# A selective scan's projections as high and low parts in float32r passes, with d, u and gate projected once

## The chip, the cores and the metric

The kernel runs on one core of one Trainium2 chip. The metric is the device time of one execution in microseconds (us). The fast runs of one kernel on one chip agree here within 0.6%. PE is the matmul engine, DVE the vector engine, ACT the scalar engine, POOL the general-purpose one, SP the one that issues most transfers; PSUM is the matmuls' output memory, SBUF the main one. In the views PEld is PE's weight loads, and a q behind an engine is its sequencer. The granted clock is the share of full speed at which PE was let run, 1.00 or 0.50 at any time in these traces; a mean lies between.

## The reference, cut to what matters

Four images of 64 x 64 tokens with 96 channels go through two layers. Layer 0 is a recurrence with 16 states per channel, whose coefficients are projections of the normed tokens; layer 1 is an attention without a softmax and a quantized feed-forward.

```python
proj = layernorm(groupnorm(x)) @ W_in + b_in             # 96 -> 3*96 + 3*96*16
value, gate, delta, A, Bm, Cm = split(proj)              # u, gate, d; a, b, c per channel and state
# over the 4096 tokens of an image, one after the other:
h = d * (A_t * h) + d * (B_t * u)
y = sigmoid(gate) * sum_over_states(C_t * h)
x = x + y @ W_out + b_out
# layer 1
t = x + attention(layernorm(x));  t = t + feed_forward(layernorm(t))
```

## The kernel before

The 4096 tokens of an image are 8 chunks of 512. A chunk's channels are 3 groups of 32, and a group's 16 states are 4 tiles of (4 states x 32 channels) = 128 partitions by 512 tokens. Per tile there are three projections (a, b, c) and one scan on DVE.

```python
def conv_main(b, i, cg):                       # one group of channels of one chunk
    d_ps = proj(pab, w_d[:, cg, :], "dps", "pab");  nc.scalar.copy(d_sb, d_ps)
    u_ps = proj(pab, w_u[:, cg, :], "ups", "pab")
    nc.vector.tensor_tensor(du, u_ps, d_sb, ALU.mult)
    for sh in range(NSH):                      # 4 tiles of states
        b_ps = proj(pab, w_b[:, cg, sh, :], f"bps{sh}", "pab")
        nc.scalar.copy(bu[:, sh, :], b_ps)
        nc.gpsimd.tensor_tensor(bu[:, sh, :], bu[:, sh, :], du, ALU.mult)
    for sh in range(NSH):
        a_ps = proj(...);  nc.vector.tensor_tensor(da, a_ps, d_sb, ALU.mult)
        nc.vector.tensor_tensor_scan(h[:, sh, :], da, bu[:, sh, :], state, ALU.mult, ALU.add)
        c_ps = proj(...);  nc.vector.tensor_tensor(ch[:, sh, :], c_ps, h[:, sh, :], ALU.mult)
    nc.gpsimd.tensor_tensor(ch[:, 0:2, :], ch[:, 0:2, :], ch[:, 2:4, :], ALU.add)
    nc.gpsimd.tensor_tensor(ys, ch[:, 0, :], ch[:, 1, :], ALU.add)
    # [cut: the state of the last token]

for g in range(N + NCH):                       # schedule; the framework may still reorder
    conv_gate(g); conv_main(g, 0)
    conv_tail(g - 1)                           # output projection, layer norm, Gram matrix
    conv_main(g, 1)
    attn_ffn(of the image before)              # layer 1 of one chunk
    # [cut: loads; in the seventh chunk gn_var, the next image's group-norm statistics]
    conv_front(g + 1)                          # group norm, layer norm, transpose of the next chunk
    conv_main(g, 2)
```

Of the kernel before, what the change touches and what calls it, by code (L numbers as in the profile page):

```python
# [8 lines left out]
F32 = mybir.dt.float32  # L9
F16 = mybir.dt.float16  # L10
F8 = mybir.dt.float8e5  # 5 exponent bits, 2 mantissa bits, infinities: the reference's q_mul
# [4 lines left out]
P = 128  # L16
B, H, W, C = 4, 64, 64, 96
L = H * W                # tokens per image
S = 16                   # states per channel
CA = C + 1               # channels and the row (or column) of ones that carries the biases  # L20
J = 4                    # token 4p + j of a chunk lies on partition p
TC = P * J               # tokens per chunk
NCH = L // TC            # chunks per image
NCG = C // 32            # groups of 32 channels
NSH = S // 4             # groups of 4 states; a scan tile has (state in group, channel in group) on partitions
G = 32                   # groups of the group norm
# [9 lines left out]
def conv_attn_hybrid_kernel(  # L36
# [24 lines left out]
    work = ctx.enter_context(tc.tile_pool(name="work", bufs=2))  # L61
# [6 lines left out]
    # x and out: token b*L + i*TC + J*p + j  # L68
# [9 lines left out]
    def load_x(b, i):  # L78
        t = big.tile([P, J, C], F32, tag="x", name=f"x_{b}_{i}", bufs=2 * NCH + 3)
        nc.sync.dma_start(t, x_v[b, i])  # L80
        xt[b, i] = t
# [12 lines left out]
    # sel[p, cg, c] = 1 where c == 32 cg + p % 32: sums the states of each channel  # L94
# [9 lines left out]
    # D ** -0.5 on the diagonal blocks of the heads, 0 elsewhere  # L104
# [17 lines left out]
    w_b = const.tile([CA, NCG, NSH, P], F32, name="w_b")  # L122
    w_a = const.tile([CA, NCG, NSH, P], F32, name="w_a")
    w_c = const.tile([CA, NCG, NSH, P], F32, name="w_c")
    w_d = const.tile([CA, NCG, P], F32, name="w_d")
    w_u = const.tile([CA, NCG, P], F32, name="w_u")
    w_g = const.tile([CA, C], F32, name="w_g")
    raw = work.tile([CA, A0], F32, tag="h", name="raw0")
    nc.scalar.dma_start(raw[0:C, :], w_in[:, 0:A0])
    nc.scalar.dma_start(raw[C:CA, :], b_in[0:A0].unsqueeze(0))  # L130
    for dst, c0 in ((w_d, 2 * C), (w_u, 0)):
        nc.vector.tensor_copy(
            dst.rearrange("k g (s c) -> k g s c", s=4),
            raw[:, c0 : c0 + C].rearrange("k (g c) -> k g c", g=NCG)
            .unsqueeze(2).to_broadcast([CA, NCG, 4, 32]),
        )
    nc.vector.tensor_copy(w_g, raw[:, C : 2 * C])
    for k, (dst, c0) in enumerate(((w_b, B0), (w_a, A0), (w_c, C0))):
        raw = work.tile([CA, C * S], F32, tag="bu", name=f"raw_{c0}")
        nc.scalar.dma_start(raw[0:C, :], w_in[:, c0 : c0 + C * S])  # L140
        nc.scalar.dma_start(raw[C:CA, :], b_in[c0 : c0 + C * S].unsqueeze(0))
        for cg in range(NCG):
            o = dst[:, cg].rearrange("k h p -> k (h p)").rearrange("k (s c) -> k s c", s=S)
            i_ = raw[:, cg * 32 * S : (cg + 1) * 32 * S].rearrange("k (c s) -> k s c", s=S)
            if (k + cg) % 2:
                nc.vector.tensor_copy(o, i_)
            else:
                nc.scalar.copy(o, i_)
# [10 lines left out]
    # [Wq; bq] transposed, with a unit row that passes bff through  # L159
# [14 lines left out]
    w1_sb = work.tile([P, NK, C], F32, tag="d", name="w1_sb")  # L174
    nc.scalar.dma_start(w1_sb, w1.rearrange("(m p) k -> p m k", p=P))
    w2_sb = work.tile([C, HID], F32, tag="du", name="w2_sb")
# [9 lines left out]
    b1_sb = work.tile([NK, P], F32, tag="da", name="b1_sb")  # L186
# [3 lines left out]
    b1_8 = work.tile([P, NK], F8, tag="xq", name="b1_8")  # L190
    nc.vector.tensor_copy(b1_8, b1_ps, saturate=False)
    nc.vector.tensor_copy(b1_q, b1_8)
    b2_sb = work.tile([P, C], F32, tag="da", name="b2_sb")
    nc.scalar.dma_start(b2_sb, b2.partition_broadcast(P))
    b2_8 = work.tile([P, C], F8, tag="xq", name="b2_8")
# [4 lines left out]
    xnt_t, yg_t, xa_t = [], [], []  # L200
    for r in range(2):
        t = const.tile([CA, TC], F32, tag=f"xnt{r}", name=f"xnt{r}")
        nc.gpsimd.memset(t[C:CA, :], 1.0)
        xnt_t.append(t)
        t = const.tile([CA, TC], F32, tag=f"yg{r}", name=f"yg{r}")
        nc.gpsimd.memset(t[C:CA, :], 1.0)
        yg_t.append(t)
        t = const.tile([P, J, CA], F32, tag=f"xa{r}", name=f"xa{r}")
        nc.gpsimd.memset(t[:, :, C:CA], 1.0)
        xa_t.append(t)  # L210

    def rsqrt(dst, var, eps):
        """dst = (var + eps) ** -0.5"""
        nc.gpsimd.tensor_scalar(dst, var, eps, None, ALU.add)
        nc.gpsimd.tensor_tensor(dst, dst, mhalf[:, : dst.shape[1]], ALU.pow)  # L215

    def layer_norm(dst, src, eps, nm):
        """Per token over the channels; src [P, J, C], dst may be src."""
# [15 lines left out]
    gnm, gnr, gn = {}, {}, {}  # L234
    inv_n = 1.0 / (L * GR)

    def group_sum(ps, dst):
        """Sum over a chunk's J tokens and each group's channels."""
        nc.vector.tensor_reduce(
            dst, ps.rearrange("p (j g r) -> p g j r", j=J, g=G), AX.XY, ALU.add  # L240
        )
# [13 lines left out]
    def gn_var(b):  # L255
        ps = pm.tile([P, J * C], F32, tag="pm", name=f"gnq_{b}")
        for i in range(NCH):
            t = big.tile([P, J, C], F32, tag="gn", name=f"gn_{b}_{i}", bufs=NCH + 2)
# [6 lines left out]
            sq = work.tile([P, J * C], F32, tag="sq", name=f"sq_{b}_{i}")  # L265
            nc.scalar.activation(sq, t.rearrange("p j c -> p (j c)"), AF.Square)
            nc.tensor.matmul(ps, lhsT=ones, rhs=sq, start=(i == 0), stop=(i == NCH - 1))
            gn[b, i] = t
# [8 lines left out]
    def conv_front(b, i):  # L277
        """Group norm, layer norm and transpose of a chunk."""
        t = gn.pop((b, i))
# [8 lines left out]
        for j in range(J):  # L288
            nc.tensor.transpose(ps[:, j, :], t[:, j, :], ident)
        xnt = xnt_t[(b * NCH + i) % 2]  # L290
        nc.scalar.activation(
            xnt[0:C, :].rearrange("c (p j) -> c j p", j=J), ps, AF.Identity,
            bias=bet, scale=gam,
        )

    gate, ysum, state = {}, {}, {}

    def conv_gate(b, i):
        xnt = xnt_t[(b * NCH + i) % 2]
        ps = pab.tile([C, TC], F32, tag="pab", name=f"g_ps_{b}_{i}")  # L300
        nc.tensor.matmul(ps, lhsT=w_g, rhs=xnt, start=True, stop=True)
        g = work.tile([C, TC], F32, tag="gate", name=f"gate_{b}_{i}")
        nc.scalar.activation(g, ps, AF.Sigmoid)
        gate[b, i] = g

    def conv_main(b, i, cg):
        """The recurrence of 32 channels over a chunk."""
        nm = f"{b}_{i}_{cg}"
        xnt = xnt_t[(b * NCH + i) % 2]

        def proj(pool, wt, n, tag):
            ps = pool.tile([P, TC], F32, tag=tag, name=f"{n}_{nm}")
            nc.tensor.matmul(ps, lhsT=wt, rhs=xnt, start=True, stop=True)  # L313
            return ps

        d_ps = proj(pab, w_d[:, cg, :], "dps", "pab")
        d_sb = work.tile([P, TC], F32, tag="d", name=f"d_{nm}")
        nc.scalar.copy(d_sb, d_ps)  # L318
        u_ps = proj(pab, w_u[:, cg, :], "ups", "pab")
        du = work.tile([P, TC], F32, tag="du", name=f"du_{nm}")  # L320
        nc.vector.tensor_tensor(du, u_ps, d_sb, ALU.mult)  # L321

        bu = work.tile([P, NSH, TC], F32, tag="bu", name=f"bu_{nm}")
        for sh in range(NSH):
            b_ps = proj(pab, w_b[:, cg, sh, :], f"bps{sh}", "pab")
            nc.scalar.copy(bu[:, sh, :], b_ps)  # L326
            nc.gpsimd.tensor_tensor(bu[:, sh, :], bu[:, sh, :], du, ALU.mult)  # L327

        h = work.tile([P, NSH, TC], F32, tag="h", name=f"h_{nm}")
        ch = work.tile([P, NSH, TC], F32, tag="ch", name=f"ch_{nm}")  # L330
        st = state.get((b, cg))
        for sh in range(NSH):
            a_ps = proj(pab, w_a[:, cg, sh, :], f"aps{sh}", "pab")
            da = work.tile([P, TC], F32, tag="da", name=f"da{sh}_{nm}")
            nc.vector.tensor_tensor(da, a_ps, d_sb, ALU.mult)  # L335
            nc.vector.tensor_tensor_scan(  # L336
                h[:, sh, :], da, bu[:, sh, :],
                0.0 if st is None else st[:, sh : sh + 1], ALU.mult, ALU.add,
            )
            c_ps = proj(pc, w_c[:, cg, sh, :], f"cps{sh}", "pc")  # L340
            nc.vector.tensor_tensor(ch[:, sh, :], c_ps, h[:, sh, :], ALU.mult)  # L341
        if i < NCH - 1:
            st = small.tile([P, NSH], F32, tag=f"state{cg}", name=f"state_{nm}", bufs=2)
            nc.scalar.copy(st, h[:, :, TC - 1])
            state[b, cg] = st
        nc.gpsimd.tensor_tensor(ch[:, 0:2, :], ch[:, 0:2, :], ch[:, 2:4, :], ALU.add)  # L346
# [176 lines left out]
```

## Time and profile before

The median of the runs taken beside the changed kernel is 2299.5 us (2295.5 to 2304.3), the profiled execution 2306.4 us. By the scans' starts it falls into these stages:

| stage | us |
|---|---|
| to the first scan | 72.6 |
| image 0, eight chunks | 469.2 |
| images 1 to 3, 24 chunks | 1637.8 |
| after the last scan | 126.8 |

The groups that the argument turns on, from the list of costliest groups (count, busy time in all, mean ns of one, then the idle time ahead of them and what ended it):

```profile
L327 POOL TENSOR_TENSOR bu<-bu,du 128x512 f32<-128x512 f32 x384 | 514.7, 1369 | 108.3 <-ACT bu L326 108.1
L336 DVE TENSOR_TENSOR_SCAN h<-da,state,bu 128x512 f32<-128x512 f32 x336 | 478.3, 1423 | 48.4 <-POOL bu L327 35.9
L313 PE MATMUL bps<-xnt,w_b 97*128 97x512 f32 x768 | 401.2, 653 | 0.5 <-DVE du L321 0.3
```

A scan's mean of 1423 ns is a mixture: 1.27 us when it starts with POOL idle (median of 294) and 1.87 us when it starts with POOL active (median of 90). All 82 scans of over 1.4 us end 1.08 us after the end of a POOL instruction (1.078 to 1.086).

### The profile page before, as it was taken

The page shows a single profiled execution, that of the slowest core. Times are in us where ns is not written, and L with a number is a line of the kernel's source. Part 1 is how long each engine was busy: PE and PEld are TensorE (multiplying, and loading weights), DVE is VectorE, ACT ScalarE, POOL GpSimd, SP SyncE. Part 2 cuts the span into 40 slices and gives each one's busy share as a digit, 9 for nine tenths or more (in the row PEclk, how much of TensorE's full clock was granted, in tenths as well). Part 3 has the DMA queues.
Part 4 walks back from the last instruction along what each step waited for, and adds up shares of the span by engine and source line. Part 5 has one row for each costly group of instructions (what it writes and reads, how often), then busy time and mean ns, then how long its engine had stood idle before and what let it go on. Part 6 is the DMA issues. An engine that isn't in the chain of part 4 may idle for free.

```text
span 2306.4 us, 15368 instructions
## 1 busy us (share of the span) xinstructions
PE 1828.3 (79%) x4744; PEld 836.0 (36%) x4744; DVE 1555.9 (67%) x2674; ACT 527.9 (23%) x891; POOL 1117.5 (48%) x898
## 2 busy tenths in 40 slices
PE   2888888878888888878888888887888788888644
PEld 1333333433333333423333333333333333333322
DVE  1677777566777777656767677764776767777633
ACT  1222211211222222222212222212222122222123
POOL 4555545754545445564444554555544454554311
PEclk9899989988988989988889898987988898888755
DMA  3000000000000000000000000000000000000000
GB/s 107 1 0 0 0 0 1 0 0 0 7 7 7 7 1 7 7 7 7 1 7 7 7 7 7 4 0 4 4 4 4 0 4 4 4 4 4 4 11 17
DMA packets 10983, 16.00 MB, mean 7 GB/s; under 512 B 2124, under 2 KB 10609, under 8 KB 10900
## 3 DMA queue, kind: packets, MB, share of 16 engines
q1 hardware_dynamic: 9216, 12.59, 1.7%
q10 hardware_dynamic: 1684, 2.43, 0.4%
q8 instruction: 37, 0.61, 0.1%
q14 instruction: 46, 0.38, 0.1%
HBM read 8.72 MB, written 6.29 MB: 7 GB/s over the span
## 4 chain that ended last, share of the span: by engine, by line
DVE 39%; PE 30%; POOL 14%; issue 11%; ACT 3%; DVEq 0%; POOLq 0%; ACTq 0%
DVE h L336 13%; DVE da L335 6%; PE bps L313 6%; DVE gn L228 5%; DVE xa L228 5%; PE aps L313 5%; DVE ch L341 4%; PE cps L313 4%; PE o_ps L366 3%; POOL ch L346 3%; POOL bu L327 2%; PE y_ps L357 2%; POOL ys L348 2%; PE dps L313 1%; POOL rstd_f L215 1%
## 5 line engine op out<-in xcount | busy, mean ns | idle before, releaser
L313 PE MATMUL cps<-xnt,w_c 97*128 97x512 f32 x768 | 445.2, 664 | 172.0 <-DVE ch L341 171.9
L327 POOL TENSOR_TENSOR bu<-bu,du 128x512 f32<-128x512 f32 x384 | 514.7, 1369 | 108.3 <-ACT bu L326 108.1
L346 POOL TENSOR_TENSOR ch<-ch 128x1024 f32<-128x1024 f32 x96 | 225.5, 2348 | 599.9 <-DVE ch L341 599.9
L336 DVE TENSOR_TENSOR_SCAN h<-da,state,bu 128x512 f32<-128x512 f32 x336 | 478.3, 1423 | 48.4 <-POOL bu L327 35.9
L313 PE MATMUL aps<-xnt,w_a 97*128 97x512 f32 x768 | 445.2, 664 | 0.0
L335 DVE TENSOR_TENSOR da<-aps,d 128x512 f32<-128x512 f32 x384 | 258.6, 674 | 243.7 <-PE aps L313 243.7
L313 PE MATMUL bps<-xnt,w_b 97*128 97x512 f32 x768 | 401.2, 653 | 0.5 <-DVE du L321 0.3
L326 ACT COPY bu<-bps 128x512 f32<-128x512 f32 x384 | 224.7, 585 | 389.3 <-PE bps L313 385.0
L313 PEld LDWEIGHTS cps<-xnt,w_c 97*128 97x128 f32 x768 | 147.8, 210 | 409.9 <-DVE ch L341 291.7
L341 DVE TENSOR_TENSOR ch<-cps,h 128x512 f32<-128x512 f32 x384 | 262.5, 684 | 19.0 <-PE cps L313 1.0
L313 PEld LDWEIGHTS aps<-xnt,w_a 97*128 97x128 f32 x768 | 162.5, 215 | 202.3 <-issue 188.6
L313 PEld LDWEIGHTS bps<-xnt,w_b 97*128 97x128 f32 x768 | 149.9, 207 | 171.3 <-issue 114.8
L457 POOL TENSOR_TENSOR o<-x,yb 128x384 f32<-128x384 f32 x32 | 50.9, 1589 | 292.1 <-DVE yb L453 292.1
L228 DVE TENSOR_SCALAR gn<-gn,mv_c,rstd_c 128x96 f32<-128x96 f32 x128 | 127.3, 1054 | 35.9 <-POOL rstd_c L215 35.9
L228 DVE TENSOR_SCALAR xa<-x,mv_a,rstd_a 128x96 f32<-128x96 f32 x128 | 121.6, 1010 | 29.3 <-POOL rstd_a L215 29.3
L318 ACT COPY d<-dps 128x512 f32<-128x512 f32 x96 | 56.5, 588 | 336.4 <-PE dps L313 336.1
L425 PE MATMUL xq_ps<-ident,xn 128*96 128x128 f32 x128 | 37.8, 394 | 109.3 <-DVE xn L228 109.3
L348 POOL TENSOR_TENSOR ys<-ch 128x512 f32<-128x512 f32 x96 | 121.6, 1266 | 5.5
L375 PE MATMUL gram<-xa 128*97 128x97 f32 x256 | 57.6, 344 | 79.2 <-DVE xa L228 79.2
L357 PE MATMUL y_ps<-ys,sel 128*96 128x512 f32 x192 | 107.1, 701 | 5.7 <-POOL ys L348 5.7
L313 PE MATMUL dps<-xnt,w_d 97*128 97x512 f32 x192 | 105.1, 630 | 0.0
L313 PE MATMUL ups<-xnt,w_u 97*128 97x512 f32 x192 | 102.3, 615 | 0.4
(120 smaller groups left out, 1595.3 us busy)
## 6 DMA issues: line engine op xcount, KB each, us to landing
x<-in_x_dram SPq DMA_DIRECT2D x32, 192.0 KB, 5.4
out_dram<-o SPq DMA_DIRECT2D x32, 192.0 KB, 1.8
raw<-in_L_conv_W_in_dram ACTq DMA_DIRECT2D x3, 576.0 KB, 5.5
w_sb<-in_L_ffn_W_dram ACTq DMA_DIRECT2D x2, 144.0 KB, 2.2
raw<-in_L_conv_W_in_dram ACTq DMA_DIRECT2D x1, 108.0 KB
w_qkv<-in_L_attn_Wqkv_dram ACTq DMA_DIRECT2D x1, 108.0 KB, 2.5
raw<-in_L_conv_b_in_dram ACTq DMA_DIRECT2D x3, 6.0 KB
b_sb<-in_L_ffn_b_dram ACTq DMA_DIRECT2D x1, 48.0 KB
```

Source lines behind the costliest of these rows:

```text
L228: nc.vector.tensor_scalar(dst[:, j, 0:C], src[:, j, :], mv[:, j, 0:1], rstd[:, j : j + 1], ALU.subtract, ALU.mult,)
L313: nc.tensor.matmul(ps, lhsT=wt, rhs=xnt, start=True, stop=True)
L326: nc.scalar.copy(bu[:, sh, :], b_ps)
L327: nc.gpsimd.tensor_tensor(bu[:, sh, :], bu[:, sh, :], du, ALU.mult)
L335: nc.vector.tensor_tensor(da, a_ps, d_sb, ALU.mult)
L336: nc.vector.tensor_tensor_scan(h[:, sh, :], da, bu[:, sh, :], 0.0 if st is None else st[:, sh : sh + 1], ALU.mult, ALU.add,)
L341: nc.vector.tensor_tensor(ch[:, sh, :], c_ps, h[:, sh, :], ALU.mult)
L346: nc.gpsimd.tensor_tensor(ch[:, 0:2, :], ch[:, 0:2, :], ch[:, 2:4, :], ALU.add)
L348: nc.gpsimd.tensor_tensor(ys, ch[:, 0, :], ch[:, 1, :], ALU.add)
L357: nc.tensor.matmul(y_ps, lhsT=sel[:, cg, :], rhs=ysum.pop((b, i, cg)), start=(cg == 0), stop=(cg == NCG - 1),)
L366: nc.tensor.matmul(o_ps[:, j, :], lhsT=yg_v[:, j, :], rhs=w_o, start=True, stop=True)
L375: nc.tensor.matmul(gram[b], lhsT=xa[:, j, :], rhs=xa[:, j, :], start=(i == 0 and j == 0), stop=(i == NCH - 1 and j == J - 1),)
```

## The change

The intent is to unload PE. An fp32 product is two instructions here, 0.86 us together at full clock; a float32r pass is one. The change takes the float32r copy of a value as its high part and what remains as its low part. Activations and weights are split so, and three passes over packed operands (96 high rows and 32 low rows in one tile of 128) give the product of both parts. The bias moves from a row of ones to an ACT bias or the first operand of a fused DVE instruction. d, u and gate are projected once per chunk for all 96 channels, and DMA copies d and d*u onto the four state groups. To make room, many working tiles lose their second buffer (a tile with two buffers can be filled anew while its last content is still read).

```diff
+    def split_weights(dst, src, lo_engine):
+        nc.scalar.copy(dst[0:C, 0], src)                              # high part
+        lo_engine.tensor_tensor(dst[0:C, 1], src, dst[0:C, 0].bitcast(F32), ALU.subtract)
+        # [cut: four copies by DMA fill the packed rows]
# [cut: ten splits (nine for a, b, c, one for d, u, gate), bias rows by 36 one-column matmuls, two instructions each]
 def gn_var(b):
-            sq = work.tile([P, J * C], F32, tag="sq", name=...)       # two buffers
+            sq = work.tile([P, J * C], F32, tag="sq", name=..., bufs=1)
-            gn[b, i] = t                                              # subtracted tile kept
 def conv_front(b, i):
+        nc.gpsimd.tensor_tensor(t, xt[b, i], gnm[b], ALU.subtract)    # done again per chunk
+        nc.scalar.copy(xs[0:C, :], xn)
+        nc.vector.tensor_tensor(lo, xn, xs[0:C, :].bitcast(F32), ALU.subtract)
+        nc.sync.dma_start(xl[0:64, :], lo[0:64, :]);  nc.sync.dma_start(xl[64:P, :], lo[0:64, :])
+        nc.sync.dma_start(xs[C:P, :], lo[64:C, :])
+    def project(pool, tag, nm, b, i, wt, m):
+        for n, mv in enumerate((xs, xs, xl)):
+            nc.tensor.matmul(ps, lhsT=wt[:, n], rhs=mv, start=(n == 0), stop=(n == 2))
 def conv_gate(b, i):
+        # d = ACT(dps + bias); du = DVE((ups + bias) * d); gate = sigmoid(gps + bias)
+        for cg in range(NCG):
+            for nm, src in (("d4", d), ("du4", du)):
+                for s in range(4):
+                    nc.sync.dma_start(t[s * 32 : (s + 1) * 32, :], src[cg * 32 : (cg + 1) * 32, :])
# [cut: conv_main: bu, h, ch as single tiles; da and ch fused with the bias; ys by three POOL additions]
 # schedule
-            conv_gate(b, i)
             conv_main(b, i, 0)
 ...
             conv_front(*divmod(g + 1, NCH))
+            conv_gate(*divmod(g + 1, NCH))
         if g < N:
             conv_main(b, i, 2)
```

## The prediction

> **What bounds the kernel now.** I read the page's busy table first, then the slices, then the stages by windows, then the timelines of single engines inside one chunk.

> ```profile
> span 2306.4 us, 15368 instructions
> PE 1828.3 (79%) x4744; PEld 836.0 (36%) x4744; DVE 1555.9 (67%) x2674; ACT 527.9 (23%) x891; POOL 1117.5 (48%) x898
> DVE 39%; PE 30%; POOL 14%; issue 11%; ACT 3%; DVEq 0%; POOLq 0%; ACTq 0%
> ```

> No engine is full, and the chain that ended last passes through DVE, PE and POOL by turns: the kernel is a relay. So the question is not which engine the change unloads but which hand-overs it shortens.

> The timeline of VectorE gives the stages by the scans' starts. The first scan starts at 72.6 us, the ninth chunk's first at 541.8, the last scan ends at 2179.6. That is a prologue of 72.6 us, image 0 with 469 (eight chunks), images 1 to 3 with 1638 (24 chunks, now with the attention and feed-forward of the image before), and a tail of 127. One ordinary chunk of image 2 runs from 1231.9 to 1298.2. The windows view cut at its scans (columns: us, then PE, PEld, DVE, ACT, POOL busy, the granted clock, DMA share and GB/s):

> ```profile
> 1231.90:1242.30 10.40, 7.86 (x19) 2.91 (x18) 10.15 (x10) 0.01 (x1) 4.54 (x3) 1.00 0.00 0
> 1242.30:1258.80 16.50, 13.74 (x38) 7.66 (x37) 8.11 (x18) 3.70 (x7) 9.82 (x8) 0.79 0.00 1
> 1258.80:1267.60 8.80, 7.92 (x25) 3.77 (x24) 8.59 (x11) 0.57 (x2) 0.00 (x0) 1.00 0.00 0
> 1267.60:1281.90 14.30, 10.84 (x26) 4.27 (x24) 10.07 (x29) 4.69 (x10) 10.92 (x10) 0.88 0.00 1
> 1281.90:1291.70 9.80, 7.20 (x27) 3.38 (x27) 9.70 (x14) 3.56 (x4) 1.09 (x1) 0.83 0.00 0
> 1291.70:1298.20 6.50, 6.50 (x17) 2.91 (x16) 2.12 (x5) 3.27 (x7) 6.26 (x5) 1.00 0.21 61
> 1231.90:1298.20 66.30, 54.07 (x144) 24.91 (x143) 48.74 (x83) 15.81 (x27) 32.63 (x26) 0.90 0.02 6
> ```

> Rows 1, 3 and 5 are the recurrences of the three channel groups: DVE is nearly full there (29 us). Rows 2, 4 and 6 lie between them (37.3 us): there POOL makes the next b*u, PE the projections, and layer 1 and the norms pass. The recurrence itself is DVE-bound; the other half of the chunk is chains.

> The second thing to see is what POOL does to DVE. First a scan with POOL busy, then POOL at that time, then a scan with POOL idle:

> ```profile
> 1095.22 2.27 DVE L336 TENSOR_TENSOR_SCAN h<-da,bu 128x512 f32<-128x512 f32 x1 [0.34 <-POOL bu L327]
> ...
> 1093.91 5.86 POOL L327 TENSOR_TENSOR bu<-bu,du 128x512 f32<-128x512 f32 x4
> ...
> 1061.59 1.28 DVE L336 TENSOR_TENSOR_SCAN h<-da,state,bu 128x512 f32<-128x512 f32 x1
> ...
> 1070.09 1.03 POOL L215 TENSOR_TENSOR rstd_f<-rstd_f,mhalf 128x4 f32<-128x4 f32 x1
> 1071.15 1.05 DVE L228 TENSOR_SCALAR xn<-x,mv_f,rstd_f 128x96 f32<-128x96 f32 x4 [3.25 <-POOL rstd_f L215]
> ...
> 1073.82 4.93 POOL L327 TENSOR_TENSOR bu<-bu,du 128x512 f32<-128x512 f32 x4
> 1073.88 4.94 DVE L228 TENSOR_SCALAR gn<-gn,mv_c,rstd_c 128x96 f32<-128x96 f32 x4 [0.88 <-POOL rstd_c L215]
> ```

> Four normalisations take 1.05 us alone and 4.94 beside four POOL products: each waits for one product to end. Of all scans, the 90 that start with POOL active have a median of 1.87 us and end 1.08 us after POOL's instruction; the other 294 take 1.27. A product is 1.26 us alone.

> [...]da and ch, which have one input in PSUM, stay near 0.68 us. [...]The trace has fp32, two instructions per product, a product every 0.86 us at full clock[...]. [...]the trace has 684 for ch. [...]the trace has 1.8 us for a 192 KB store and 0.34 us of issue each.

> **The change part by part.**
> PE. Before, each channel group makes 14 projections: 14 x 0.86 = 12.0 us, three times a chunk, plus the gate: 37 us. [...]But PE is waited on only at hand-overs, so what this is worth depends on the order.
> DVE. du falls from three to one (-1.2 us), lo is added (+0.6), the rest keeps its count. POOL: three adds of 1.26 (3.8) for 2.35 + 1.27 (3.6), one group-norm subtraction more (0.9). ACT: one copy more (0.6), states in four pieces. DMA: 24 copies of 64 KB and three for the split, 27 x 0.35 = 9.5 us of issue per chunk on SP, otherwise idle.
> The order, which the instruction lists of both kernels show, matters more. (a) Gap between groups 0 and 1: before, the projections of group 1 stood behind the output projection and the Gram matrix on PE; now they stand ahead, and group 1's b*u is made during group 0. 16.5 us shrinks to ch, ch, yg, da: 2.6. (b) Gap from group 2 to the next chunk: 6.5 shrinks to about 2.4, since the next b*u is made early. (c) Gap between groups 1 and 2: before, the norm of the next chunk ran under group 2. Now du of the next chunk stands ahead of group 2 on DVE, and dps, ups, gps ahead of group 2's projections on PE. So everything up to du becomes one serial chain.
> The chain (c), from the last scan of group 1: residual add and ch 1.15, statistics 1.0, POOL add and rstd_f to 3.9, xn 1.05, statistics, rstd_c to 7.1, gn beside two POOL group-norm steps to 9.9, hr 1.05, hq 1.5, y_ps 1.1, y16 0.5, yb 0.55: 14.8 us. (The tail runs this feed-forward part alone in 12.0 us from add to yb.) ACT xn 1.27 and the high part 0.6 after y16: 16.2; lo 0.65: 16.9; SP issues three copies, the third lands at 19.6. Then, at half clock at first, [...]d 0.6, [...]du 0.7, gps, bps, aps with three PSUM buffers: first scan at 27.7 us, against 14.3.
> The recurrences. POOL's work no longer has its own gaps: about 18 of its 21 long instructions per chunk now fall among the 12 scans. [...]18 x 1.23 + 12 x 1.08 + rstd_a 1.3 + xa 1.05 = 37.5 us; DVE alone would need 31. [...]
> Period: 27.7 + 37.6 = 65.3, against 66.3: -1.0, or -24 us over 24 chunks. Image 0 has no feed-forward: chain (c) is about 20, so 57.7 against 57: +3 in all. The chunk that holds the next image's statistics took 87.6 and 90.2 us in images 1 and 2; eight group-norm products in a row (6.9 us) leave it, the single square buffer lengthens it: -18. Prologue: nine weight splits of copy, subtraction, four copies by DMA, and one DMA more in the first chain: +10. Tail unchanged: 0. Sum: 2302 - 24 + 3 - 18 + 10 = 2273, say 2275.

> **The rivals.**
> 1. The relay wins. [...]recurrences come near 33 us, and landing is shorter: 60 us a chunk, 2130 to 2160 in all. For it: DVE busy is 48.7 of 66.3 now. Against it: every long wait of a scan in the trace ends 1.08 us after POOL's instruction.
> 2. Chain (c) is longer: the chain of waits has 11% "issue", which my steps hardly hold, and PE falls to half clock between bursts (0.51 in the tail, by the windows). With 4 us more per chunk: 2400. Against it: PE [...]kept clock 1.00 in rows 1 and 3 with pauses of 1 to 2 us.
> [...]
> 4. SP stalls: the store of o and a load stand ahead of the split's copies in its list. I counted it (lo and o end within 1 us); a late o would add directly to (c).

> **Range and chances.** The period is a difference of two large moves (-18 in the short gaps, +13.4 in the long one, +8.6 in the recurrences), each uncertain by 2 to 3 us, over 32 chunks: some 90 us either way. 2275, with 2160 to 2395 eight times in ten. Faster by over 2% (below 2256) 0.42, within 0.36, slower 0.22.

> **What would show it.** Right: scans with a median near 1.9 us; gaps before groups 0 and 1 near 2.5 us and one gap near 28 before group 2; that gap ends in the split's copies by DMA, then dps; PE busy near 1400 us, POOL and DVE hardly changed. Wrong: a float32r matmul over 0.3 us apart at full clock; scans near 1.3 (rival 1); group 2 starting before du; copies landing after 3 us or more; a prologue above 95 us.

Its sum came to 2302 - 24 + 3 - 18 + 10 = 2273, said as 2275, and terms of it are cut: the rate taken for a float32r pass, which no trace had shown, and what rests on it alone, namely PE's work after the change (the 1400 us rest on it too), the d and u projections in chain (c), and rival 3 (a slower pass, 2550 us). So the terms left between the landing (19.6) and the first scan (27.7) are not all of them. The fused product was taken to last as long as ch, 0.68 us. The 37.5 us of the recurrences stand as an estimate from the traces of the kernel before: 18 POOL products of 1.23 us (four took 4.93) and 12 scans that end 1.08 us after POOL's instruction. The step from there to the 37.6 of the sum is cut, and so is the assumption of rival 1, that POOL's instructions run beside da and ch.

## The result, and the profile after

The changed kernel takes 2359.8 us (2359.0 to 2361.8, four runs) beside 2299.5 us: a ratio of 1.026, 95% interval 1.024 to 1.028. It is slower. (A ratio here is the mean time of one kernel's runs over that of the other's of the same rounds, so not quite the ratio of the medians.) The profiled execution is 51.7 us longer than that of before. By the scans' starts (the prediction doesn't say whether its -18 for the chunks with statistics holds image 0's chunk too; here all of it stands with images 1 to 3):

| stage | before | after | difference | predicted |
|---|---|---|---|---|
| to the first scan | 72.6 | 101.5 | +28.9 | +10 |
| image 0 | 469.2 | 481.6 | +12.4 | +3 |
| images 1 to 3: two chunks with statistics | 177.8 | 178.4 | +0.6 | -20 |
| images 1 to 3: the last chunk | 60.3 | 46.5 | -13.8 | -1 |
| images 1 to 3: the 21 others | 1399.7 | 1426.8 | +27.1 | -21 |
| after the last scan | 126.8 | 123.3 | -3.5 | 0 |
| sum | 2306.4 | 2358.1 | +51.7 | -29 |

The page's head of the changed kernel:

```profile
span 2358.1 us, 19871 instructions
PE 1615.1 (68%) x5808; PEld 1074.4 (46%) x5808; DVE 1480.1 (63%) x2640; ACT 594.5 (25%) x1116; POOL 1337.3 (57%) x1033
POOL 26%; PE 23%; DVE 22%; issue 15%; ACT 8%; DMA 4%; SPq 3%; POOLq 0%; ACTq 0%; DVEq 0%
```

PE was unloaded by 213 us of busy time, although the mean granted clock fell from 0.869 to 0.796, and the kernel became slower. The chain that ended last now leads through POOL most, and transfers and their issue (DMA, SPq) are in it. Where the time went inside a chunk is seen in the windows of an ordinary chunk of image 2, cut at its scans (us, then PE, PEld, DVE, ACT, POOL busy, granted clock, DMA share, GB/s); rows 1, 3 and 5 are the recurrences:

```profile
1289.73:1299.89 10.16, 7.66 (x29) 4.85 (x28) 10.16 (x10) 2.46 (x6) 6.91 (x5) 1.00 0.00 0
1299.89:1302.55 2.66, 1.96 (x8) 1.51 (x8) 2.56 (x5) 0.78 (x2) 2.66 (x3) 1.00 0.00 0
1302.55:1315.55 13.00, 8.88 (x46) 7.00 (x45) 11.86 (x24) 1.06 (x4) 8.72 (x7) 0.94 0.00 0
1315.55:1345.51 29.96, 19.64 (x63) 11.59 (x62) 9.98 (x36) 10.41 (x15) 10.94 (x12) 0.63 0.17 47
1345.51:1355.15 9.64, 6.59 (x26) 4.37 (x25) 9.64 (x10) 2.44 (x6) 8.31 (x6) 1.00 0.40 96
1355.15:1357.75 2.60, 1.90 (x8) 1.58 (x9) 2.60 (x4) 0.78 (x2) 2.60 (x3) 1.00 0.00 0
1289.73:1357.75 68.02, 46.63 (x175) 30.90 (x175) 46.80 (x82) 17.93 (x35) 40.15 (x31) 0.82 0.13 34
```

The short gaps fell from 16.5 and 6.5 us to 2.7 and 2.6, and one gap of 30 us stands ahead of group 2. No engine is busy for more than 20 of its 30 us, and its clock is 0.63: a serial chain. Its links in time order, from the timelines of that stretch:

```profile
1319.43 1.05 DVE L251 TENSOR_SCALAR xn<-x,mv_f,rstd_f 128x96 f32<-128x96 f32 x4 [1.54 <-POOL rstd_f L238]
1322.55 1.05 DVE L251 TENSOR_SCALAR gn<-gn,mv_c,rstd_c 128x96 f32<-128x96 f32 x4 [1.46 <-POOL rstd_c L238]
1326.49 1.14 PE L500 MATMUL y_ps<-w_q,hq 128*128 128x96 fp8e5 x12 [2.98 <-ACT hq L495]
1327.43 1.05 PE L317 MATMUL xnt_ps<-ident,gn 128*96 128x128 f32 x4
1330.47 1.38 DVE L326 TENSOR_TENSOR lo<-xn,xs 96x512 fp32r<-96x512 f32 x1 [1.73 <-ACT xs L325]
1333.46 0.59 SPq L329 DMA_DIRECT2D xs<-lo  x1
1335.79 1.14 PE L340 MATMUL dps<-xs,w_dug 128*96 128x512 f32 x2 [4.22 <-DMA xs<-lo]
1338.73 0.75 DVE L350 SCALAR_TENSOR_TENSOR du<-ups,b_dug,d 96x512 f32<-96x512 f32 x1 [6.88 <-PE ups L340]
1339.72 1.05 PE L340 MATMUL bps<-xs,w 128*128 128x512 f32 x2
1344.14 1.45 DVE L385 SCALAR_TENSOR_TENSOR da<-aps,b_bac,d 128x512 f32<-128x512 f32 x2 [4.66 <-PE aps L340]
1345.51 3.58 DVE L389 TENSOR_TENSOR_SCAN h<-da,state,bu 128x512 f32<-128x512 f32 x2
```

The next chunk's normed tile is ready at 1323.6, but its transposes stand on PE behind the feed-forward's y_ps (1326.5). The split's third copy is issued at 1333.5 and lands at 1335.8. PE, idle for 4.2 us, starts at half clock: two passes of bps take 1.05 us here, and from 1341.8 on 0.63. Over the 16 ordinary chunks the gap's median is 29.1 us (14.3 before); the recurrences proper went from 29.0 to 32.6 us. The groups that answer to those shown of before:

```profile
L375 POOL TENSOR_TENSOR bu<-bu,du 128x512 f32<-128x512 f32 x384 | 605.8, 1602 | 413.1 <-ACT bu L374 365.8
L389 DVE TENSOR_TENSOR_SCAN h<-da,state,bu 128x512 f32<-128x512 f32 x336 | 548.0, 1656 | 2.9
L340 PE MATMUL bps<-xs,w 128*128 128x512 f32 x768 | 288.4, 451 | 34.2 <-ACT bu L374 32.0
```

Products and scans both became longer although their work is the same: they now meet more often. 258 of the 384 scans start while POOL is active (90 before), and those have a median of 2.03 us; the others take 1.27. All 186 scans of over 1.4 us end 1.08 us after the end of a POOL instruction (1.077 to 1.089).

In the prologue the statistics' matmuls start late and form a ladder:

```profile
44.60 6.90 PE L269 MATMUL gns<-x,ones 128*128 128x384 f32 x16
53.88 1.15 PE L290 MATMUL gnq<-sq,ones 128*128 128x384 f32 x2 [2.38 <-ACT sq L289]
55.70 1.65 PE L290 MATMUL gnq<-sq,ones 128*128 128x384 f32 x2 [0.67 <-ACT sq L289]
```

In the kernel before the means (gns) started at 27.3 us, and from the first square to the last matmul it took 7.4 us; here it takes 18.0, in steps of 2.32 us: ACT's square, then a matmul, then again the one square buffer.

### The profile page after: what moved, and what is told of

The parts are those of the page before. It is cut to its first block, busy times and chain, and to the rows that moved or that the text cites. A ratio compares the mean times of both kernels' runs of the same rounds, so it can differ in the third digit from the quotient of the medians.

```text
span 2358.1 us, 19871 instructions
## 1 busy us (share of the span) xinstructions
PE 1615.1 (68%) x5808; PEld 1074.4 (46%) x5808; DVE 1480.1 (63%) x2640; ACT 594.5 (25%) x1116; POOL 1337.3 (57%) x1033
## 4 chain that ended last, share of the span: by engine, by line
POOL 26%; PE 23%; DVE 22%; issue 15%; ACT 8%; DMA 4%; SPq 3%; POOLq 0%; ACTq 0%; DVEq 0%
POOL ys L401 10%; POOL bu L375 9%; DVE h L389 8%; PE bps L340 5%; DVE da L385 3%; PE cps L340 3%; DVE ch L396 3%; DMA xs<-lo 3%; PE dps L340 2%; ACT hq L495 2%; PE gnq L290 2%; ACT bu L374 2%; PE y_ps L411 2%; ACT xn L319 2%; PE y_ps L500 1%
## 5 line engine op out<-in xcount | busy, mean ns | idle before, releaser
L375 POOL TENSOR_TENSOR bu<-bu,du 128x512 f32<-128x512 f32 x384 | 605.8, 1602 | 413.1 <-ACT bu L374 365.8
L340 PE MATMUL cps<-xs,w 128*128 128x512 f32 x768 | 305.2, 483 | 165.9 <-DVE ch L396 165.7
L385 DVE SCALAR_TENSOR_TENSOR da<-aps,b_bac,d 128x512 f32<-128x512 f32 x384 | 275.8, 736 | 156.9 <-PE aps L340 129.3
L401 POOL TENSOR_TENSOR ys<-ys,ch 128x512 f32<-128x512 f32 x192 | 312.6, 1628 | 36.1 <-DVE ch L396 32.3
L374 ACT ACTIVATE bu<-bps,b_bac 128x512 f32<-128x512 f32 x384 | 263.8, 688 | 267.9 <-PE bps L340 192.3
L340 PE MATMUL bps<-xs,w 128*128 128x512 f32 x768 | 288.4, 451 | 34.2 <-ACT bu L374 32.0
L396 DVE SCALAR_TENSOR_TENSOR ch<-cps,b_bac,h 128x512 f32<-128x512 f32 x384 | 271.5, 732 | 0.3
L340 PE MATMUL aps<-xs,w 128*128 128x512 f32 x768 | 246.3, 399 | 0.0
L340 PEld LDWEIGHTS bps<-xs,w 128*128 128x128 f32 x768 | 163.4, 213 | 104.6 <-ACT bu L374 45.6
L340 PE MATMUL cps<-xl,w 128*128 128x512 f32 x384 | 174.1, 453 | 0.0
L340 PE MATMUL bps<-xl,w 128*128 128x512 f32 x384 | 160.4, 418 | 0.0
L511 POOL TENSOR_TENSOR o<-x,yb 128x384 f32<-128x384 f32 x32 | 29.1, 909 | 130.4 <-DVE yb L507 130.4
```

The costliest lines, as they stand in the source:

```text
L340: nc.tensor.matmul(ps, lhsT=wt[:, n], rhs=mv, start=(n == 0), stop=(n == 2))
L374: nc.scalar.activation(t, b_ps, AF.Identity, bias=b_bac[:, 0, cg, sh : sh + 1])
L375: nc.gpsimd.tensor_tensor(t, t, du4, ALU.mult)
L385: nc.vector.scalar_tensor_tensor(da, a_ps, b_bac[:, 1, cg, sh : sh + 1], d4, ALU.add, ALU.mult)
L396: nc.vector.scalar_tensor_tensor(t, c_ps, b_bac[:, 2, cg, sh : sh + 1], h, ALU.add, ALU.mult)
L401: nc.gpsimd.tensor_tensor(ys, ch[0] if sh == 1 else ys, t, ALU.add)
```

## The experiments

Thirteen kernels were run. The framework orders each engine's instructions itself, so an edit can move more than it says. For the runs that hold the changed kernel's own schedule the traces were compared: how many of the 2640 DVE instructions of the changed kernel's trace stand in the same sequence (the longest common one, by operation, names without buffer numbers, and shape).

```
sq2 2634   stats_first 2629   ys1 2634   warm 2639   warm2 2640   pass1 2531   pass4 2119
```

All but ys1 were accepted by the comparison with the reference. Times are medians of four runs; each ratio is to the kernel before on the same chip. The period is the time from a chunk's first scan to the next chunk's; the 16 ordinary chunks are those of images 1 to 3 without each image's first, the two with statistics, the ones behind these, and the last.

### sq2: two square buffers

```diff
-            sq = work.tile([P, J * C], F32, tag="sq", name=f"sq_{b}_{i}", bufs=1)
+            sq = work.tile([P, J * C], F32, tag="sq", name=f"sq_{b}_{i}")
```

> The changed kernel with two buffers instead of one for the squares of the group-norm statistics; nothing else. Theory (one square buffer makes the eight steps of the statistics a ladder of 2.32 us each, ACT square 0.52 then a matmul of two instructions at half clock then the next, where before the change a step took 0.84 in the prologue): the ladder in the prologue falls from 18.0 us to about 10 (matmul-bound if the clock stays at half), and the three chunks that hold the next image's statistics lose 8 to 12 us each. In all 30 to 45 us less than the changed kernel, that is 2315 to 2330 us, ratio to before about 1.01. Rival (the ladder is set by PE at half clock, the buffer is hidden): under 10 us less, 2350 or more.

It took 2356.5 us, ratio 1.022. The first scan came at 91.7 instead of 101.5 us, so the prologue behaved as the theory said. The chunks with statistics did not: 88.9 and 91.3 us against 89.4 and 89.0, and 76.5 against 72.0 in image 0. The total lies in the rival's range, but not for its reason: the buffer did set the ladder. The timeline of such a chunk (PE, then POOL and DVE) shows why:

```profile
1027.23 7.77 PE L290 MATMUL gnq<-sq,ones 128*128 128x384 f32 x16
...
1037.20 5.46 POOL L238 TENSOR_TENSOR gnr<-gnr,mhalf 128x32 f32<-128x32 f32 x1
...
1043.77 1.02 POOL L238 TENSOR_TENSOR rstd_c<-rstd_c,mhalf 128x4 f32<-128x4 f32 x1
1044.83 1.05 DVE L251 TENSOR_SCALAR gn<-gn,mv_c,rstd_c 128x96 f32<-128x96 f32 x4 [7.95 <-POOL rstd_c L238]
```

The ladder shrank to 7.8 us, but now the power of 5.46 us for the next image stands on POOL ahead of the small power that the next chunk's norm waits for. In the changed kernel it stood behind it. The next chunk's transposes start 32.9 us after group 1's last scan; without the edit it was 33.0. The ladder ended 9 us earlier (22.6 us after that scan instead of 31.8), and all of it was given back to another wait.

### stats_first: statistics of image 0 ahead of the weight splits

```diff
+    gn_mean(0); gn_var(0)        # definitions moved up with them
     w_dug = const.tile([P, 3, 3 * C], F32R, name="w_dug")
     # [cut: the splits]
-    gn_mean(0)
-    gn_var(0)
     conv_front(0, 0)
```

> The changed kernel with the statistics of image 0 emitted ahead of the weight splits instead of after them; nothing else moves. Theory (in the prologue the mean's matmuls stand on PE behind 72 bias-row matmuls that wait for three single-partition copies of 2.72 us on POOL, so they start at 44.6 us where the kernel before starts them at 27.3): the first scan moves from 101.5 us to between 70 and 82; everything after it is shifted whole; total 2328 to 2342. Rival (the weight splits themselves, with their 36 copies by DMA, are what the first projection waits for): the first scan moves by less than 8 us.

It took 2342.7 us, ratio 1.016; the first scan came at 87.5 us, 14.0 earlier, short of the 70 to 82 expected, and the rest was shifted whole. The means now start at once:

```profile
4.68 4.10 PE L156 MATMUL gns<-x,ones 128*128 128x384 f32 x9
```

The squares then interleave with the bias-row matmuls and still end only at 49.9 us: the moved part had been waiting. That the weight splits, on the same engines, hold it up now is likely but not tested.

### gate_late and front_early: the same instructions in another order

```diff
 # gate_late                                   # front_early
     conv_main(b, i, 1)                        +    loads, gn_var; conv_front(g + 1)
     attn_ffn(...)                                  conv_main(b, i, 1)
     conv_front(g + 1)                         +    conv_gate(g + 1)
-    conv_gate(g + 1)                               attn_ffn(...)
     conv_main(b, i, 2)                        -    loads, gn_var; conv_front(g + 1); conv_gate(g + 1)
+    conv_gate(g + 1)                               conv_main(b, i, 2)
```

> The changed kernel with the d, u, gate projections and copies of the next chunk emitted after group 2 instead of before it; the norm and the split of the next chunk stay where they are. Theory (what costs is the order: everything up to du of the next chunk is one serial chain ahead of group 2): the gap before group 2 falls from 29 us to 10 to 14, the gap before the next group 0 grows from 2.6 to 9 to 12, the recurrences get a little shorter since some of POOL's products fall into that gap; period of an ordinary chunk 60 to 63 us instead of 67.7, total 2180 to 2240. Rival ([...]order only moves the waits about): period within 1 us of 67.7, total within 25 us of 2360.

> The changed kernel with the next chunk's norm, split emitted ahead of group 1, its d, u, gate after group 1, then the attention and feed-forward, then group 2: the same instructions in another order. Theory (order): the split lands during group 1, so before group 2 stand only du and the first half of the feed-forward; gaps about 12, 8 and 2.5 us instead of 2.7, 29, 2.6; recurrences 36 to 40 us in all since POOL's work has fewer gaps of its own; period 57 to 62, total 2100 to 2220. Rival[...]: period within 1 us of 67.7.

The clauses cut from the two rivals had the time of POOL's instructions and of the scans together set the period.

gate_late took 2334.3 us, ratio 1.012. In image 0 the chunks fell from 61.3 to 55.6 us, but in images 1 to 3 the period is 68.7: the gap ahead of group 2 fell to 12.0 us, the one after it rose to 16.8. The chain was cut and its second half stood open in the other place. PE has to do y_ps first, which waits for POOL's last sum, and the copies of d*u queue on SP behind those of d:

```profile
1307.74 2.02 PE L411 MATMUL y_ps<-ys,sel 128*96 128x512 f32 x2 [5.52 <-POOL ys L401]
...
1308.77 1.84 PE L340 MATMUL dps<-xs,w_dug 128*96 128x512 f32 x2
```

So the theory was wrong about this order: moving part of the chain is not enough.

front_early took 2089.4 us, ratio 0.906, below the range expected. Same parts, 11.5% less than the changed kernel. The gaps are 12.7, 11.6 and 1.6 us, near the 12, 8 and 2.5 expected; the recurrences came out shorter than the 36 to 40. An ordinary chunk of it (group 1's gap, its recurrence, group 2's gap, the whole):

```profile
1145.00:1157.66 12.66, 9.65 (x37) 8.16 (x37) 6.44 (x28) 2.05 (x4) 9.72 (x10) 0.73 0.00 0
1157.66:1167.53 9.87, 7.16 (x30) 5.14 (x29) 9.45 (x13) 2.29 (x5) 5.03 (x4) 0.83 0.15 34
1167.53:1179.08 11.55, 8.09 (x28) 5.22 (x26) 6.42 (x16) 4.79 (x8) 8.67 (x8) 0.79 0.35 86
...
1134.79:1192.86 58.07, 45.97 (x176) 31.97 (x175) 45.33 (x81) 17.73 (x35) 39.34 (x31) 0.85 0.16 41
```

The busy times of the whole chunk are those of the changed kernel within 2 us, and the chunk is 10 us shorter. The norm now lies in the first gap, the split and its copies under group 1's recurrence, and dps can start at 1165.3, before group 1's last scan. The recurrences are not longer for it (32.3 us in all, 32.6 in the changed kernel).

### b_front_early: the kernel before in that order

```diff
 # on the kernel before
+    loads, gn_var; conv_front(g + 1)
     conv_main(b, i, 1)
     attn_ffn(...)
-    loads, gn_var; conv_front(g + 1)
     conv_main(b, i, 2)
```

> The kernel before (plain fp32 projections, d and u per group) with the next chunk's norm emitted ahead of group 1 instead of ahead of group 2: the same move that made the changed kernel 9.4% faster than before, as far as the kernel before has its parts. Theory (the order is worth much only where the norm, the split, the copies and du form one chain; here group 2 waits for the feed-forward and the norm side by side): between 2230 and 2310. Rival (the order alone, and not the change, is what the fast version gains): 2090 to 2180.

It took 2318.1 us, ratio 1.009: a little slower than the kernel before and outside both ranges. In the kernel before, the order by itself gains nothing; there the norm does not lead into a split, copies and a shared du, which fits the theory, but its range was missed by 8 us. Between the two kernels in this order the whole change is worth 2318 - 2089 = 229 us.

### ys1: two of three POOL additions left out (wrong result)

```diff
-            if sh:
+            if sh == 1:
                 nc.gpsimd.tensor_tensor(ys, ch[0] if sh == 1 else ys, t, ALU.add)
```

> The changed kernel with one instead of three POOL additions per group (the sum over states keeps only the first two of four tiles); the result is wrong on purpose. It takes 2 x 3 x 1.27 = 7.6 us of POOL per chunk away, of which most lie among the scans. Theory[...]: scans with POOL active at their start fall from 258 to under 180, the recurrences with their short gaps fall from 38.4 us to 32 to 35, period 62 to 65, total 2200 to 2290. Rival (DVE's own order and PE's c projections set the recurrences; the long scans only fill waits that are there anyway): period within 1 us of 67.7.

It took 2248.9 us, ratio 0.979; the relative error of 0.59 was intended. The period fell by 3.1 us to 64.6 (means of the ordinary chunks), 2.8 us of it in the recurrences proper (medians 32.6 to 29.9). DVE is busy throughout the recurrences and its list is nearly the same (2634 of 2640), and a scan's mean fell from 1.65 to 1.52 us, so the direction is that of the theory, that waits of scans for POOL set the recurrences; the size was overrated. 205 scans still start beside POOL, where I expected under 180, and 7.6 us of POOL's work bought 3.1.

### pass1: one pass instead of three

```diff
-        for n, mv in enumerate((xs, xs, xl)):
+        last = 2 if m == C else 0              # a, b, c: one pass; d, u, gate: three
+        for n, mv in enumerate((xs, xs, xl)[: last + 1]):
```

> The changed kernel with one float32r pass instead of three for the b, a and c projections (d, u and gate keep three); the result is wrong on purpose. It takes 24 matmuls of 0.235 us per group of channels off PE, some 17 us of 46 per chunk. Theory (PE is off the path except ahead of the first scan of group 2, where four bps and one aps stand in its order after the copies): the gap before group 2 shortens by 2.5 to 3.5 us, the recurrences stay (10, 13, 9.6 us), period 64 to 65.5 instead of 67.7, total 2260 to 2290. Rival (PE bounds the recurrences): they shorten by 3 us or more besides, total below 2230. A third view (PE is off every path): within 15 us of 2360.

It took 2420.7 us, ratio 1.054: slower than the changed kernel, against all three views. (The comparison accepted it, which I had not expected: on its inputs the tolerance does not need the other two passes.) The mean granted clock fell from 0.796 to 0.613. The recurrence of group 0 in an ordinary chunk, from the windows:

```profile
1324.17:1336.07 11.90, 5.33 (x9) 2.62 (x10) 10.26 (x10) 2.06 (x6) 8.11 (x5) 0.50 0.00 0
```

With nine matmuls in 12 us PE stays at half clock even there, and what is left on PE (y_ps, o_ps, the transposes) runs at that clock; a y_ps matmul's mean rose from 878 to 1011 ns over the whole run. The long gap became 1.7 us shorter, the first gap grew from 2.7 to 6.5. 109 of DVE's 2640 instructions left their place too, so the 61 us are not all shown to be the clock's; the clock itself is shown by the row.

### warm and warm2: PE kept busy while it waits for the copies

```diff
 # warm2, in conv_gate; warm: nine such matmuls on the split of the chunk before
+        for _ in range(10):
+            nc.tensor.matmul(d_ps, lhsT=w_dug[0:C, 0, 2 * C :], rhs=xs[0:C, :], start=True, stop=True)
         d_ps = project(...)                    # overwrites d_ps
```

> The changed kernel with nine idle float32r matmuls (results overwritten) on PE ahead of the d projection of the next chunk, on the split of the chunk at hand, in the 4.2 us in which PE waits for the split's copies. Theory (the long gap was 1.6 us longer than predicted because PE's clock is granted at half from the landing of the copies until the first a projection: 5 us of work at half speed): the projections after the landing run at 0.235 us instead of 0.43, the gap before group 2 falls by 2 to 3.3 us, period 64.5 to 66, total 2255 to 2300. Rival 1 (landing to first scan is set by ACT, POOL and DVE, not by PE's speed): gap within 0.7 us, total 2340 to 2365. Rival 2 (the idle matmuls delay d themselves): slower than 2365.

> The changed kernel with ten idle float32r matmuls (overwritten) directly ahead of the d projection of each chunk, reading the first 96 rows of the new split, which are there 5.3 us before the copies land; they can only run in PE's wait for the copies. Theory (half clock after that wait lengthens the gap): d, u, gate and b projections run at 0.235 us a pass instead of 0.43, landing to first scan falls from 9.7 to 7 to 8 us, gap before group 2 from 29.3 to 26.5 to 28, total 2270 to 2330. Rival (ACT, POOL and DVE set that stretch): gap within 0.7 us, total 2340 to 2370.

warm took 2362.3 us, ratio 1.026, and tells nothing: its idle matmuls needed nothing late, so they ran early, and PE's wait for the copies stayed at 4.7 us. warm2 reads rows that only come with the new split, so its matmuls must stand in that wait. It took 2310.4 us, ratio 1.004: 49 us less than the changed kernel by work that does nothing. After the landing PE now runs at full clock:

```profile
1306.65 0.70 PE L341 MATMUL dps<-xs,w_dug 128*96 128x512 f32 x2 [1.53 <-DMA xs<-lo]
...
1308.80 0.63 PE L341 MATMUL bps<-xs,w 128*128 128x512 f32 x2
```

From here to the first scan (1313.87) are 7.2 us; in the changed kernel it was 9.7. The gap's median fell from 29.1 to 26.9, the period's from 67.6 to 65.1. DVE's sequence is that of the changed kernel, so no new order of it explains this.

### pass4 and fe_pass4: PE's cost put back

```diff
+        if m == P:
+            nc.tensor.matmul(ps, lhsT=wt[:, 2], rhs=xl, start=True, stop=True)   # overwritten
         for n, mv in enumerate((xs, xs, xl)):
```

> The changed kernel in its own order with one more idle pass in each b, a and c projection (overwritten)[...]. Theory (in this order PE's saved time is mostly hidden: it is on the path only in the long gap, with four b and one a product): gap before group 2 1 to 2 us longer, less what a higher clock gives back; period 67.5 to 70, total 2360 to 2430. Rival (PE's pace is on the path of the recurrences too, as in the early order, where the same change cost 103 us): total above 2450.

> The early order (2089 us) with one more idle float32r pass in each b, a and c projection, overwritten by the three real ones[...]; the result is unchanged. It puts 36 x 0.235 = 8.5 us of PE back per chunk. Theory (what the early order gains is not PE's saved time but d and u made once and the b*u products early; PE has slack and gets a higher clock when busier): total 2060 to 2120. Rival (the cheaper products are the gain): the difference of the two kernels in this order, 2318 to 2089, comes back for the most part: 2200 or more.

pass4 took 2515.0 us (ratio 1.093), 155 more than the changed kernel; fe_pass4 2191.8 (ratio 0.953), 102 more than front_early. Both are far over what I expected of hidden work: pass4 lies in its rival's range, fe_pass4 8 us below its own. But neither is clean. Four passes of 0.233 us are 0.93 us, more than the 0.86 of the fp32 product that they were to stand for. And the order changed: in pass4 only 2119 of 2640 DVE instructions keep their sequence, and in fe_pass4 2250 of front_early's 2640; why the framework ordered anew was not looked into. In pass4 the residual add, statistics and norm of the chunk before moved ahead of group 1, and that gap grew from 2.7 to 10.5 us, while the long gap, where the theory puts PE's cost, grew by 0.8. The mean granted clock rose with PE's work, from 0.796 to 0.829 in pass4 and from 0.847 to 0.887 in fe_pass4. So PE's saved time seems to be worth something in both orders; how much of these sums is PE's own, and how much the reordering's, stays open.

### both_fixes and late_var: towards a better version

both_fixes is front_early with stats_first and two square buffers. late_var is that, with gn_var emitted last in the seventh chunk:

```diff
             conv_main(b, i, 2)
+        if b + 1 < B and i == NCH - 2:
+            gn_var(b + 1)
```

> The changed kernel in the early order (norm and split ahead of group 1, d, u, gate after it) with the statistics of image 0 ahead of the weight splits and with two square buffers. Theory: the early order gave 2089; the prologue loses 14 us as it did by the moved statistics alone and up to 8 more by the second buffer; the chunks with the next image's statistics stay within 3 us each, since there the 5.5 us power on POOL took the place of the ladder. Total 2062 to 2080. Rival (the gains overlap, the prologue is then bound by the weight splits): 2080 to 2090.

> Both fixes and the early order as in the run both_fixes (2084 us), with the squares of the next image's statistics emitted after group 2 of the seventh chunk of an image instead of ahead of its norm. Theory (in those three chunks the eight steps of the statistics, 10 to 18 us, and the 5.5 us power stand in the order of POOL and PE ahead of the norm of the next chunk; 79 to 85 us against 51 and 58): those chunks and the ones after them lose 15 to 25 us together each time, total 2010 to 2045. Rival (POOL's 14 us of statistics delay the b*u products wherever they stand): 2065 to 2090.

both_fixes took 2083.8 us, ratio 0.907, no better by the ratio than front_early. The prologue lost 17.9 us, but image 0 grew by 7.5 and images 1 to 3 by 5.4: the statistics' ladder and power again, 79.3 us instead of 72.1 in the chunk of image 0. late_var took 2038.7 us (2035.1 to 2039.0), ratio 0.886, interval 0.883 to 0.888. The chunks with statistics fell from 84.7 to 73.4 us in images 1 and 2 and from 79.3 to 60.6 in image 0. It beats both kernels: 11.4% less than the kernel before.

## Why the prediction was wrong

It said 2275 us, 1% faster; the kernel is 2.6% slower. The range held it, the direction did not. Taken by the prediction's own steps:

- **The shape of a chunk was right.** The gaps ahead of groups 0 and 1 were predicted at 2.4 and 2.6 and are 2.6 and 2.7. The chain (c) ends in the split's copies and dps, as said. The recurrences with their short gaps were predicted at 37.6 us; they are 37.9 (32.6 + 2.7 + 2.6, medians), or 38.5 by means. The range's three moves (-18, +13.4, +8.6) add to +4.0 and not to the forecast's -1.0: the 37.6 holds the two short gaps already, so the recurrences proper were to move by 3.6, as they did. float32r ran one pass per 0.233 us, so the sign of over 0.3 us did not come.
- **The scans' median was wrong as worded.** It is 1.28 us, near the 1.3 that was named as a sign for rival 1. Only some scans of a group are held up: the medians of the four are 2.05, 2.21, 1.27, 1.75 in group 0, 1.98, 1.28, 1.27, 1.27 in group 1 and 1.51, 2.22, 1.27, 2.27 in group 2. The mean rose from 1.42 to 1.65, and the sum of 37.6 was nevertheless near; rival 1's 33 was not.
- **The gap (c) was mis-sized: 27.7 predicted, 29.1 measured.** Up to lo the chain ran to the sum: 16.9 predicted, 16.3 measured (in part by luck: the high part came 1.3 us early, and lo took 1.38 us for 0.65). The copies landed at 19.7 (median of the 16 chunks; 20.2 in the one shown) for 19.6, though SP needs about 0.6 us to issue one and 0.35 was taken. The term that failed is the last one, from landing to the first scan: 8.1 predicted, 9.7 measured. "At half clock at first" was right, but the prediction gave it the d projection alone; in the chunk shown it lasts 5.5 us (1335.8 to 1341.3, clock 0.50), through d, u, gate and the first b projections. warm2 shows it: with PE at full clock this stretch takes 7.2 us and the period becomes 65.1, against 65.3 predicted. 13 of the 16 chunks start dps at half clock, after waits of 3.1 to 4.4 us, and the other three, after 2.7 to 3.3 us, fall to half within 0.4 us; in the chunk shown of warm2 the wait is 1.53 us and dps runs at full clock (0.70 us for two passes, 1.14 in the changed kernel). Waits of that length do not account for all of the gap, though: in the chunk shown the clock is at half from 1314.0 to 1331.0 already, and PE had no pause over 1.7 us in the 6.8 us before that. Of the 16 gaps, 68 to 76% of the time is at half clock, and warm2 mends only the end (the mean clock over the gap is 0.71 in its chunk, 0.63 in that of the changed kernel). Rival 2 had named the half clock and put 4 us on it; 2.2 were there.
- **Two busy times were wrong.** PE was predicted near 1400 us and is 1615. A pass takes longer than was taken (117 passes in each of 32 chunks), and the clock is lower (0.796 for 0.869); what each makes of the difference was not taken apart. POOL was to change hardly and rose from 1117 to 1337: each product takes 1602 ns for 1369 (+89 us), each of the three sums 1.60 us for the 1.26 taken (+98), both beside DVE's scans (the 280 products and sums that start within a scan have a median of 2.18 us, the other 392 of 1.29); the second subtraction (+29) had been counted.
- **Image 0 was mis-sized the same way:** its gap is 22.8 us, where "about 20" was written without a sum. warm2 takes 2.4 of it back. (The +3 is no sum of its chunks either: 57.7 against 57 is +5.6 in eight.)
- **The prologue was mis-sized: +10 predicted, +28.9 measured.** Nine splits were counted (there are ten), but not what stands behind them: image 0's statistics, worth 14.0 us (stats_first). The one square buffer is worth 9.8 (sq2); together 17.9 (both_fixes), for the two overlap. What is left, 11, is near the forecast's 10. Its sign of being wrong, a prologue above 95 us, came true (101.5).
- **The statistics' chunks failed: -18 predicted besides each chunk's -1, +0.6 measured.** The step counted eight POOL products that leave and named the single buffer without a number. The products left (the gap behind group 2 fell there from 21.6 to 2.6 us in image 1), but the gap ahead of group 2 became 51.3 us, against 29.1 in an ordinary chunk. The buffer alone is not the cause, as sq2 shows; the statistics lie in one order with the next norm on POOL and PE, and late_var, which moves them, takes 11 to 19 us off such a chunk, though in the early order and not in this one.
- **The last chunk (-13.8) and the end (-3.5) were not told apart.** The long chain isn't there when no next chunk follows; I counted it as an ordinary one.

The direction was missed by these terms together, 81 us off: ordinary chunks +48, statistics' chunks +21, prologue +19, image 0 +9, less 16 for the last chunk and the end. Why the change does not pay is another question. Each step took the order of the changed kernel as given, and within it the forecast of a chunk was within 2.4 us. The expected gain went into that order: everything up to du of the next chunk was made one serial chain ahead of group 2, and front_early, with the same instructions, is 270 us faster. That is no error of the sum, which had the chain in it; it was accepted and not questioned. The waits of scans for POOL are real: ys1 took 7.6 us of POOL's work off a chunk and won 3.1, the order 9.6. What these waits cost in all stays open. Of the tiles that lost their second buffer only the squares' was tested; front_early keeps the others single, so they do not stand in the way of its 270 us.

## What to carry to other kernels

When a change turns parallel preparation into a chain (norm, split, copy, project, copy), ask first where that chain begins in each engine's order, and start it one stage earlier; here that was worth 270 us, where the change as it stood cost 60. Work taken off PE is not free time: where PE then waits more, its clock can fall (0.796 to 0.613 in pass1) and what is left runs longer. And after each experiment look at whether the order of instructions held, since one edit can move a fifth of them (pass4).
